# Part of block 1's front end and block 2's statistics issued inside the hand-ordered head of a Mamba + MoE kernel, with a new table of ranks

## The chip, the cores and the metric

The kernel runs on one core of one Trainium2 chip. The metric is the device time of one execution in microseconds (us). One execution is also recorded by the hardware profiler; its span, from the first to the last instruction, is what the profile's times are counted from.

The engines are called as the profile calls them: PE multiplies matrices (PEld is its weight load, which overlaps), DVE is the vector engine, ACT the scalar engine, POOL the GpSimd engine, SP the queue that issues most DMAs.

## What is computed

The input x has 4 sequences of 512 tokens with 256 features, all float32. In short:

```
x = x + layernorm(mamba(layernorm(x)))
x = x + layernorm(moe(layernorm(x)))

mamba(h):   xi, gate = split(h @ in_proj)                 # 512 channels each
            xi  = silu(causal_conv4(xi) + b)
            ts, B, C = split(xi @ x_proj)                 # 16, 16, 16
            dt  = softplus(ts @ dt_proj + dt_b)           # 512 channels
            s_t = s_{t-1} * exp(dt_t * A) + dt_t * B_t * xi_t   # 512 channels x 16 states
            y_t = sum_state(s_t * C_t)
            return ((y + D * xi) * silu(gate)) @ out_proj

moe(h):     top 4 of 16 experts by softmax(h @ w_router), weights renormalised
            out = shared/5 + (4/5) * sum_e cw_e * (silu(h@we1_e) * (h@we3_e)) @ we2_e
```

The kernel computes every expert for every token and multiplies by a weight that is zero for the experts not chosen; the shared network is cut into 4 more "experts" of the same size, so there are 20 of 128 hidden units each.

## The kernel before

**Blocks.** The 2048 tokens are cut into 8 blocks of 256 (n = 0 to 7); two blocks make one sequence, so the odd blocks continue the state and the convolution of the block before. Every block goes through four parts.

- The front (function front): statistics of x on DVE, reciprocal deviation on POOL (rstd_of, L380: four small instructions), normalisation on ACT (two instructions, L391), transposes on PE and their eviction on ACT, the projections `in` (two halves m = 0, 1) and `gin` (the gate, two halves), the convolution as matmuls with diagonal weights (`conv`), sigmoid on ACT and silu on DVE, `x_proj`, `ssm`, `dt`, softplus on ACT (a table load before and after it), and the DMAs that spread dt and dt*x over the layout of the scan.
- The scan: 32 slots per block, numbered k = 0 to 255 over all blocks. A slot has `exps` on ACT (three instructions), `scan` (L824) and `hc` (L832) on DVE and, in even blocks, `keep` on ACT. Every second slot has one `dbx` on POOL (L541). Every four slots have one `sum` on PE: 8 matmuls at L846 that read the four `hc` tiles. Two sums fill one PSUM tile, then `close` on DVE (L858) reads it.
- The chain: output projection (`out0`, `out`), layer norm, residual, second layer norm, transposes, router, top 4, and a DMA of the expert weights. It lies on all engines in turn.
- The experts, two at a time, 10 sets per block, numbered i = 0 to 79 over all blocks: `h1` and `h3` (4 matmuls each, L1088), `act` on ACT, `gated` on DVE (L1107), `weighted` and `product` on POOL, and `down` (4 matmuls, L1123).

**Who orders the work.** Each engine runs its instructions in the order in which the program issues them. The first part of the program is written out by hand: DMA issues, then function first() (L545 to L620), which takes block 0 as far as the inputs of slots 0 to 3. Everything after that is a list of tasks that class Plan puts in order with its own durations and dependencies. A task's rank is its nominal place plus a shift from the table SHIFTS (by kind and block) plus an entry of NUDGES (by task); PATIENCE lets a task of better rank go ahead of one that could start sooner. So the three tables decide the order of every engine from there on. Work that first() has already done is told to the planner with did(), with the buffers that it holds.

**Fillers.** warm(n, bank) issues n matmuls of a 128x128 identity that nobody reads. There are 20 at the start, 8 in the rest of first() (4 and 2 around x_proj, 2 before the spread at L607), and until the first `down` one group before each PE task whose planned start is late:

```python
spare_n = int((t["start"] - end - 0.4) / 0.22)
if early and spare_n > 1:
    warm(spare_n, "po")
```

**Buffers that matter here.** PSUM has three banks `h` for the scan (ps_e) and one each for f, y, h1, h3, po. In SBUF the ring `g` (3 buffers, 128x512) belongs to the experts, `o` (1 buffer) to the chain, `hc` has 11 buffers, `dbx` 3.

Of the kernel before, what the change touches and what calls it, by code (L numbers as in the profile page):

```python
# [14 lines left out]
P = 128  # L15
# [42 lines left out]
    fA=(-2, -14.75, -1.5, -59.5, 52, 5.75, 37.75, 15),  # L58
    fB=(20.5, -5, 12.5, 6.25, 26.25, 45.25, 0, -46),
    fC=(7.75, 2, -31, -1.5, 13.5, 14, -33.5, 18),  # L60
    fD=(12, 34.75, 16.5, 0.25, -2.5, 39.25, 8, 11.25),
    exps=(5.75, 36.5, 17.25, -3.75, -60, 51.75, 2, 37.75),
    dbx=(6.5, 1.25, -27.75, -13.5, -14.25, 5.25, 14.25, 46.5),
    scan=(33.75, 18.75, -5.75, 40.75, 52.75, 51.5, 57.25, -15.75),
    hc=(-4.75, -60, 50.25, -27, 28.5, 59.25, 16.75, 26.75),
    keep=(58, 0, -5.75, 0, 52, 0, 14.5, 0),
    sum=(60, -12.75, 1.25, 31.25, 16.5, 7, 0.5, -43.25),
    close=(-4.75, 27.5, 5.5, -13.75, -3, 20, 15, 36.5),
    ld=(1.5, 29.25, 27, -3, 15.75, -7.5, 57.5, -5.25),
    bc=(5, 3, 5.25, 6, 10.5, 15.75, 0.75, -3.25),  # L70
    chain=(-26, -5.25, -55, -60, -6, -38.25, -22.75, 0.25),
    load=(-5.5, 34, -50.25, 21.25, -21.25, -44, 2.75, 5.5),
    h1=(45.5, 3, -35.75, 8.25, 25.75, -0.5, 14.75, 34.5),
    h3=(11.25, -3, -53.5, -26, -29.25, -19, -15.75, -4),
    act=(-6.25, 40.25, 5.5, -11.5, -31.5, 0, 0, -3.25),
    gated=(-2, -9.5, -4.5, -23.25, 11.75, -60, -3, 0),
    prod=(33, -50, 58.75, -60, -50.75, -26.25, -8.75, 0),
    down=(-18.75, 25.5, -45, 42.25, -60, -14, 0.75, 37),
    fin=(14.75, -3, 27.75, 59, 0.5, 59.5, 3.5, -4),
# [3 lines left out]
    fA=(1.5, 0.1, 0.1, 0.3, 0.1, 1, 0.3, 0.1),  # L83
    fB=(2.2, 0.1, 0.1, 0.3, 0.1, 2.2, 0.6, 0.6),
    fC=(0.3, 0.1, 0.3, 1, 0.1, 0.6, 0.3, 0.3),
    fD=(2.2, 0.1, 0.1, 0.1, 0.1, 0.1, 0.1, 0.6),
    exps=(0.1, 0.1, 0.6, 0.1, 1.5, 0.3, 1.5, 0.3),
    dbx=(0.1, 0.3, 0.1, 0.1, 0.1, 0.1, 1, 1.5),
    scan=(0.1, 0.1, 0.1, 0.6, 0.1, 0.1, 0.1, 0.1),
    hc=(0.1, 0.1, 0.6, 1.5, 2.2, 0.1, 2.2, 0.1),  # L90
    keep=(0.1, 0.1, 0.1, 0.1, 0.6, 0.1, 0.1, 0.1),
    sum=(2.2, 0.1, 0.1, 0.1, 2.2, 0.1, 0.1, 0.1),
    close=(0.1, 0.1, 0.6, 1, 0.3, 0.3, 0.6, 1.5),
    ld=(1.5, 0.3, 1.5, 0.3, 0.1, 0.1, 0.1, 1.5),
    bc=(0.6, 0.1, 0.1, 1, 1, 0.1, 0.1, 0.3),
    chain=(0.6, 0.6, 0.1, 0.6, 0.6, 1, 0.1, 2.2),
    load=(2.2, 1, 0.6, 1, 2.2, 2.2, 0.6, 0.1),
    h1=(0.3, 0.3, 0.3, 0.1, 0.1, 0.1, 0.3, 0.1),
    h3=(0.1, 0.3, 2.2, 0.1, 0.1, 1, 0.6, 0.1),
    act=(0.6, 2.2, 0.1, 0.3, 0.1, 0.1, 0.6, 2.2),  # L100
    gated=(0.6, 0.3, 1, 0.1, 0.6, 0.1, 0.1, 1),
    prod=(2.2, 0.1, 0.1, 0.1, 0.1, 0.3, 0.1, 1.5),
    down=(0.1, 0.1, 0.1, 1.5, 0.1, 0.3, 0.1, 0.3),
    fin=(0.3, 0.3, 0.1, 1.5, 0.1, 1, 1, 0.3),
# [3 lines left out]
    ("gin", 0, 0): 5.5, ("pad0", 1, 0): 5.75, ("in", 1, 0): 3, ("xg", 1, 0, 1): 8,  # L108
    ("inputs", 1, 0): 8, ("gate", 1, 0): 14.5, ("evict", 2): 16.5, ("conv", 2, 1): -5.5,
    ("inputs", 2, 0): -27.75, ("pad0", 3, 1): -8, ("conv", 3, 1): 19.25, ("silu", 3, 1): -21.25,  # L110
    ("conv", 4, 0): 25, ("xg", 4, 0, 1): 7.5, ("gin", 4, 1): -27, ("gsig", 4, 1): 18.25,
    ("gate", 4, 1): 9.75, ("x_proj", 5): -1, ("in", 6, 1): -19.75, ("stats", 7): 5.5,
    ("conv", 7, 1): -22.5, ("x_proj", 7): 9.5, ("gin", 7, 0): 12.5, ("dbx", 2): -10,
    ("keep", 6): -14.25, ("keep", 9): -3, ("hc", 11): -1.75, ("keep", 11): -2.5,
    ("keep", 13): 13, ("dbx", 8): 32.75, ("keep", 16): -12, ("keep", 20): -21.25,
    ("scan", 21): 7, ("close", 6): -6, ("decay0", 7): -5, ("sum", 14): -3, ("yg", 7): -0.5,
    ("reps", 10): 12.5, ("hc", 84): 12.75, ("exps", 95): 10, ("exps", 96): -6.25,
    ("scan", 99): -7.75, ("sum", 24): -3, ("decay0", 13): 9.5, ("scan", 106): -3,
    ("sum", 27): -10, ("scan", 112): -14.75, ("scan", 118): 62, ("scan", 122): -3.5,
    ("scan", 125): -6.25, ("scan", 126): 2, ("scan", 138): -8.75, ("keep", 140): -4.75,  # L120
    ("scan", 144): 2.25, ("keep", 146): 27.25, ("scan", 157): 5.75, ("scan", 162): 23.25,
    ("dbx", 84): -4.75, ("decay0", 22): 4.5, ("scan", 179): 53.75, ("dbx", 91): 8.75,
    ("yg", 22): 57, ("scan", 196): -17.5, ("scan", 201): -0.25, ("reps", 26): 6,
    ("scan", 210): 11.25, ("scan", 214): -9, ("scan", 217): 6, ("sum", 54): 3.25,
    ("dbx", 110): -13, ("scan", 223): -8, ("delta", 28): 8.5, ("yg", 28): 24.5,
    ("scan", 235): -2.75, ("close", 29): 8, ("scan", 246): 48.75, ("scan", 252): -1.25,
    ("out0", 0): 35.5, ("rstd2", 0): -27.5, ("w13", 2): -3.75, ("cwb", 2): 15.75,
    ("h3", 3): 26.5, ("w13", 5): 14.75, ("product", 5): -7, ("w2", 6): -15, ("w13", 7): 4,
    ("gated", 7): -2, ("cwb", 9): 19, ("frstd", 0): -20.75, ("fadd", 0): 9.75,
    ("turnw", 1): 8.25, ("w13", 10): -12, ("h1", 10): 11.5, ("act", 15): -17.75,  # L130
    ("weighted", 17): -31.75, ("h3", 18): 3, ("down", 25): 17.75, ("cwb", 26): 10.75,
    ("down", 28): -9, ("h1", 29): -12.75, ("h1", 31): 8, ("down", 33): -14.5,
    ("act", 37): 15.25, ("add1", 4): 13.5, ("act", 46): -14.5, ("w13", 48): 9.5,
    ("share", 5): -10.75, ("cwb", 53): -4, ("h3", 54): 19, ("cwb", 54): -27.5,
    ("down", 54): -5.75, ("w2", 55): 2, ("h1", 55): -5, ("w2", 56): 2.5, ("w2", 58): 16,
    ("cwb", 59): -7.25, ("add1", 6): 8, ("down", 63): 15, ("h1", 67): -13.5, ("h1", 79): 3.25,
    ("fstats", 7, 1): -5, ("fadd", 7, 0): 8.75,
# [143 lines left out]
def mamba_then_moe(ctx: ExitStack, tc: tile.TileContext, a: dict, out: bass.AP):  # L281
# [17 lines left out]
    def load_x(n, what=xs, nm="x"):  # L299
        what[n] = work.tile([P, NU, D], F32, name=nm, bufs=RINGS[nm])  # L300
        nc.sync.dma_start(out=what[n], in_=x_in[:, n])
# [8 lines left out]
    nc.sync.dma_start(out=chan, in_=a["chan"].rearrange("(c p) k -> p c k", p=P))  # L310
    w_x = const.tile([P, CI, P // 2], F32, name="w_x")
# [17 lines left out]
    for n in range(1, 3):  # L329
        load_x(n)  # L330
# [92 lines left out]
    def in_proj(n, m, bank):  # L423
        t = q["in", n, m] = ps.tile([P, 2, U], F32, name=bank)
        for j in range(2):
            for k in range(CD):
                T.matmul(  # L427
                    t[:, j, :], w_in[:, k, ts(2 * m + j, P)], q["xn_t", n][:, k, :],
                    start=k == 0, stop=k == CD - 1,
                )  # L430

# [113 lines left out]
    def first():  # L545
# [5 lines left out]
        for i in range(NU):  # L551
            V.tensor_scalar(
                xn[:, i, :], xs[0][:, i, :], st[:, i, 1:2], rstd[:, i : i + 1],
                ALU.subtract, ALU.mult,
            )
        xn_t = q["xn_t", 0] = ring(work, [P, CD, U], "xn_t")
# [5 lines left out]
        make_taps()  # L562
        for m in range(2):
            in_proj(0, m, ("h3", "y")[m])
# [7 lines left out]
        for m in range(2):  # L572
            conv(0, m, (("po", "f"), ("h1", "h3"))[m])
        sigmoid(0, 0)
        silu(0, 0)

# [5 lines left out]
        silu(0, 1)  # L582
        S.activation(spare, zero, AF.Softplus)
        x_proj(0, "y", lambda c: warm(5 - c, "f"))
# [10 lines left out]
        warm(2, "y")  # L595
# [46 lines left out]
    for m in range(2):  # L642
        add(("xg", 0, 0, m), "SP", 0.9, 4.0 + m, lambda m=m: to_xg(0, 0, m, q["xt", 0, m]),
            (), (), [("xt", 0, m)], 256)
    did(("bc", 0), [("bt", ("bt", 0)), ("ct", ("ct", 0))])
# [9 lines left out]
    def front(n, at, over):  # L655
# [8 lines left out]
        def key(nm, *m):  # L664
            return (nm, n) + m
# [16 lines left out]
        if n:  # L682
# [3 lines left out]
            def stats():  # L686
                mine["mv"] = stats_of(xs[n])
# [28 lines left out]

            def pad0(m):
                xp = q["pad", n, m] = ring(work, [P, 2, KC - 1 + U], "xp")
                if n % UB:
                    G.tensor_copy(xp[:, :, 0 : KC - 1], tails.pop((n, m)))  # L720
                else:
                    G.memset(xp[:, :, 0 : KC - 1], 0.0)
# [7 lines left out]
            for m in range(2):  # L730
                ends = (n + 1) % UB
                starts = n % UB
                once(key("pad0", m), "POOL", 0.12, lambda m=m: pad0(m),
                     [("tail", n - 1, m)] if starts else [], [("xp", key("xp", m))],
                     [("tail", n, m)] if starts else [])
# [590 lines left out]
```

## Time and profile before

| | |
|---|---|
| median of 4 runs | 694.47 us (694.02 to 694.68) |
| profiled execution, its own time | 694.6 us |
| span of the profiled execution | 692.5 us |
| busy: PE / DVE / POOL / ACT | 675.7 / 578.2 / 602.3 / 493.4 us |
| first scan starts, first expert matmul starts | 27.71 us, 120.00 us |
| last matmul ends | 687.5 us |
| one group of 4 expert matmuls (two records each) | 1.73 us |
| one scan; one hc, busy | 1220 ns; 680 ns |

A busy PE is not a PE that does needed work: the fillers count as busy, too (216 records for 108 of them at L349 in banks f and po, and 4 for 2 in bank y). Matmul records overlap, so the pace is read from one group's start to the next. The DMAs of 256 KB land some 4.5 us after their issue, most of them hidden.

### The profile page before, as it was taken

What the parts mean: (1) busy time and instruction counts of PE and PEld (TensorE: products, weight loads), DVE (VectorE), ACT (ScalarE), POOL (GpSimd) and SP (SyncE); (2) the same over time, 40 slices, a digit from 0 to 9 for tenths busy, and PEclk for the clock granted to TensorE, in tenths of its full rate; (3) what the DMA queues carried; (4) which work ended last, traced back from release to release, by engine and by line L of the source; (5) the groups of instructions that cost most, each with busy time, mean ns of one, the idle gap of its engine ahead of it and who ended that gap; (6) DMA issues with size and microseconds to landing.
All of it is one profiled execution on the core that took longest, in us unless ns stands there. A gap on an engine that the chain in (4) does not pass through costs nothing.

```text
span 692.5 us, 13366 instructions
## 1 busy us (share of the span) xinstructions
PE 675.7 (98%) x4480; PEld 539.5 (78%) x4480; DVE 578.2 (83%) x821; ACT 493.4 (71%) x1308; POOL 602.3 (87%) x607
## 2 busy tenths in 40 slices
PE   8999998999999999999999999999999999999997
PEld 7876776767878678887787787787877787888886
DVE  3698999999999899999999999889999979952112
ACT  2799979988778778877798857877778657733311
POOL 1598669999999999999999999999999999985553
PEclk9999999999999999999999999999999999999999
DMA  5397765586866686777668766788776656463560
GB/s 175 115 337 241 258 238 191 191 268 199 288 233 222 211 303 215 232 262 279 217 226 279 245 222 226 213 291 288 244 245 227 235 192 213 139 228 131 189 228 29
DMA packets 84840, 155.28 MB, mean 224 GB/s; under 512 B 9858, under 2 KB 33410, under 8 KB 84772
## 3 DMA queue, kind: packets, MB, share of 16 engines
q1 hardware_dynamic: 83940, 153.13, 65.8%
q10 hardware_dynamic: 832, 1.31, 0.5%
q8 instruction: 35, 0.57, 0.3%
q14 instruction: 33, 0.27, 0.1%
HBM read 135.40 MB, written 19.01 MB: 223 GB/s over the span
## 4 chain that ended last, share of the span: by engine, by line
PE 62%; DVE 13%; ACT 10%; POOL 8%; DMA 3%; issue 3%; SPq 0%; DVEq 0%; POOLq 0%
PE h L1088 30%; PE po L1123 14%; DVE h L824 6%; PE y L846 6%; POOL dbx L541 4%; ACT h L529 4%; DVE hc L832 3%; PE f L941 3%; PE f L427 2%; PE f L442 2%; PE f L1123 1%; PE f L349 1%; DMA xg<-gate 1%; DVE gate L786 1%; POOL g L1110 1%
## 5 line engine op out<-in xcount | busy, mean ns | idle before, releaser
L824 DVE TENSOR_TENSOR_SCAN h<-h,dbx 128x512 f32<-128x512 f32 x256 | 307.4, 1220 | 11.7 <-ACT h L532 5.9
L541 POOL TENSOR_TENSOR dbx<-rep,bt 128x1024 f32<-128x1024 f32 x127 | 300.1, 2366 | 12.6 <-DVE h L824 12.4
L1088 PE MATMUL h<-xn_t,w 128*128 128x256 f32 x1280 | 295.2, 382 | 0.1
L529 ACT ACTIVATE h<-rep,a_rep 128x256 f32<-128x256 f32 x512 | 244.6, 478 | 53.2 <-DVE hc L832 41.4
L1088 PEld LDWEIGHTS h<-xn_t,w 128*128 128x128 f32 x1280 | 239.5, 190 | 42.7 <-issue 4.0
L832 DVE TENSOR_TENSOR hc<-h,ct 128x512 f32<-128x512 f32 x256 | 169.9, 680 | 2.9 <-ACT carry L836 0.7
L1123 PE MATMUL po<-w,g 128*128 128x256 f32 x600 | 143.7, 382 | 1.0 <-POOL g L1110 1.0
L1123 PEld LDWEIGHTS po<-w,g 128*128 128x128 f32 x600 | 111.7, 190 | 22.3 <-POOL g L1110 3.7
L1110 POOL TENSOR_TENSOR g<-g,q 128x512 f32<-128x512 f32 x80 | 102.0, 1274 | 9.0 <-DVE q L1107 7.1
L1107 DVE SCALAR_TENSOR_TENSOR q<-th,h 128x512 f32<-128x512 f32 x80 | 54.4, 680 | 49.5 <-PE h L1088 41.2
L1103 POOL TENSOR_TENSOR g<-g,cwb 128x512 f32<-128x512 f32 x64 | 81.7, 1276 | 14.5 <-ACT g L1100 13.9
L1095 ACT ACTIVATE th<-h 128x512 f32<-128x512 f32 x80 | 47.6, 595 | 46.7 <-PE h L1088 46.5
L846 PE MATMUL y<-hc,sel 128*32 128x256 f32 x1024 | 67.7, 385 | 0.0
L846 PEld LDWEIGHTS y<-hc,sel 128*32 128x32 f32 x1024 | 27.4, 109 | 28.6 <-issue 14.5
L532 ACT COPY h<-zero 128x1 f32<-128x1 f32 x256 | 41.7, 163 | 8.2
L427 PE MATMUL f<-xn_t,w_in 128*128 128x256 f32 x176 | 42.5, 384 | 1.6 <-DVE gate L786 1.1
L1100 ACT COPY g<-h 128x512 f32<-128x512 f32 x64 | 37.1, 580 | 8.7 <-PE f L1123 8.7
L427 PEld LDWEIGHTS f<-xn_t,w_in 128*128 128x128 f32 x176 | 32.7, 190 | 9.1 <-DVE gate L786 1.7
L836 ACT COPY carry<-h 128x2 f32<-128x2 f32 x128 | 19.6, 159 | 15.3 <-DVE hc L832 7.6
L442 PE MATMUL h<-xp,taps 64*64 64x256 f32 x288 | 29.5, 381 | 0.8 <-DVE xt L459 0.8
L941 PE MATMUL f<-w_out,yg 128*128 128x256 f32 x112 | 26.7, 384 | 0.2 <-DVE xt L459 0.2
L442 PE MATMUL f<-xp,taps 64*64 64x256 f32 x208 | 25.3, 382 | 0.7 <-DVE gate L786 0.4
(178 smaller groups left out, 631.4 us busy)
## 6 DMA issues: line engine op xcount, KB each, us to landing
w<-in_w SPq DMA_DIRECT2D x80, 512.0 KB, 4.8
rep<-rep SPq DMA_DIRECT2D x124, 256.0 KB, 4.5
w<-in_w SPq DMA_DIRECT2D x80, 256.0 KB, 4.5
cwb<-cwd SPq DMA_DIRECT2D x64, 256.0 KB, 4.9
xg<-xg SPq DMA_DIRECT2D x32, 256.0 KB, 4.7
bt<-bc SPq DMA_DIRECT2D x8, 512.0 KB, 6.0
ct<-bc SPq DMA_DIRECT2D x8, 512.0 KB, 6.2
xg<-gate SPq DMA_DIRECT2D x16, 256.0 KB, 4.3
```

The costliest lines, as they stand in the source:

```text
L427: T.matmul(t[:, j, :], w_in[:, k, ts(2 * m + j, P)], q["xn_t", n][:, k, :], start=k == 0, stop=k == CD - 1,)
L442: T.matmul(t[j][half[r ^ j], :], taps[half[r], 2 * m + j, k, :], q["pad", n, m][half[r], j, k : k + U], start=k == 0, stop=k == KC - 1,)
L529: S.activation(h[:, j, :], dt[:, m, 0, :], AF.Exp, scale=a_rep[:, c, g, m : m + 1])
L541: G.tensor_tensor(t[:, m], reps[n * CI + c][:, m, 1, :], bt[:, m], ALU.mult)
L824: V.tensor_tensor_scan(flat, flat, dbx[:, ts(p, NJ), :].rearrange("p j t -> p (j t)"), 0.0, ALU.mult, ALU.add)
L832: V.tensor_tensor(hc, expo[k], ct, ALU.mult)
L846: T.matmul(ys[n, c][m * CS : (m + 1) * CS, :], sel, hcs[k][:, j, :], start=g == 0, stop=g == SG - 1,)
L1088: T.matmul(t[:, j, :], weights[i][:, j, ts(CD * w + k, P)], x[:, k, :], start=k == 0, stop=k == CD - 1,)
L1103: G.tensor_tensor(gs[i], gs[i], cws[i], ALU.mult)
L1107: V.scalar_tensor_tensor(t, hid[i, "th"], 1.0, hid[i, 1], ALU.add, ALU.mult)
L1110: G.tensor_tensor(gs[i], gs[i], hid[i, "q"], ALU.mult)
L1123: T.matmul(acc[n][t] if n == N - 1 else acc[n][:, t, :], gs[i][:, j, ts(t, P)], weights2[i][:, j, :], start=m == 0 and j == 0 and (t == 0 ...
```

## The change

Four things are edited by hand, and the three tables (SHIFTS, PATIENCE, NUDGES) are replaced as a whole.

1. The load of block 1's x is issued third on SP, ahead of four loads of weights, where it was ninth.
2. first() now also does, for block 1: statistics (DVE), reciprocal deviation (POOL), normalisation (ACT), transposes (PE) into an `h` bank, their eviction on DVE (it was ACT) into a buffer of ring `g`, the projection `in` half 0 (PE; two matmuls in the place of four fillers between the halves of x_proj, two in the place of two fillers behind dt's projection), its copy into the padded tile on DVE (it was ACT), and the two copies of the convolution's tail on POOL. It also takes block 2's statistics (DVE).
3. These tasks leave the planned part: for block 1 stats, rstd, norm, transpose, evict, both pad0, in half 0 and its copy; for block 2 the task stats stays but issues nothing.
4. The number of fillers is 109 where it was 110: 22 in the hand-written part (28 before) and 87 in the planned part (82 before).

The counts of matmuls other than fillers are the same in both programs. The orders of all engines behind first() differ throughout, since the tables differ.

```diff
 SHIFTS = dict(
...
-    scan=(33.75, 18.75, -5.75, 40.75, 52.75, 51.5, 57.25, -15.75),
+    scan=(30.75, 59, -4.25, 58.25, 59, 55.75, 19.5, -8.5),
...
-    sum=(60, -12.75, 1.25, 31.25, 16.5, 7, 0.5, -43.25),
+    sum=(-4.75, 3.5, -4.5, 1.5, 11.75, 24.5, -21.25, 0.5),
...
@@ the DMA issues ahead of the program
     nc.sync.dma_start(out=chan, in_=a["chan"].rearrange("(c p) k -> p c k", p=P))
+    load_x(1)
     w_x = const.tile([P, CI, P // 2], F32, name="w_x")
...
-    for n in range(1, 3):
-        load_x(n)
+    load_x(2)
...
-    def in_proj(n, m, bank):
-        t = q["in", n, m] = ps.tile([P, 2, U], F32, name=bank)
+    def in_parts(n, m, t):
+
+        q["in", n, m] = t
         for j in range(2):
             for k in range(CD):
                 T.matmul(
                     t[:, j, :], w_in[:, k, ts(2 * m + j, P)], q["xn_t", n][:, k, :],
                     start=k == 0, stop=k == CD - 1,
                 )
+                yield
+
+    def in_proj(n, m, bank):
+        for _ in in_parts(n, m, ps.tile([P, 2, U], F32, name=bank)):
+            pass
...
@@ first()
+
+        mr = rstd_of(stats_of(xs[1]))
         xn_t = q["xn_t", 0] = ring(work, [P, CD, U], "xn_t")
...
         make_taps()
+        xn1 = ring(work, [P, NU, D], "o")
+        normalize(xn1, tiles_of(xs[1]), mr)
...
         for m in range(2):
             conv(0, m, (("po", "f"), ("h1", "h3"))[m])
+        t = ps_e.tile([P, CD, U], F32, name="h")
+        for k in range(CD):
+            for i in range(NU):
+                T.transpose(t[:, k, ts(i, P)], xn1[:, i, ts(k, P)], ident)
         sigmoid(0, 0)
         silu(0, 0)
+
+        q["xn_t", 1] = ring(work, [P, CD, U], "g")
+        V.tensor_copy(q["xn_t", 1], t)
...
         silu(0, 1)
+
+        live[2]["mv"] = stats_of(xs[2])
+        parts = in_parts(1, 0, ps_e.tile([P, 2, U], F32, name="h"))
+        for m in range(2):
+            xp = q["pad", 1, m] = ring(work, [P, 2, KC - 1 + U], "xp")
+            G.tensor_copy(xp[:, :, 0 : KC - 1], tails.pop((1, m)))
+
+        def some(c):
+            if c == 1:
+                next(parts)
+                next(parts)
+            else:
+                warm(2, "f")
+
         S.activation(spare, zero, AF.Softplus)
-        x_proj(0, "y", lambda c: warm(5 - c, "f"))
+        x_proj(0, "y", some)
...
         V.tensor_copy(first_b, b0)
-        warm(2, "y")
+        for _ in parts:
+            pass
+        V.tensor_copy(q["pad", 1, 0][:, :, KC - 1 :], q["in", 1, 0])
         softplus(0)
...
+    did(("evict", 1), [("g", ("xn_t", 1))], eng="DVE")
+    for m in range(2):
+        did(("pad0", 1, m), [("xp", ("xp", 1, m))], [("tail", 1, m)], eng="POOL")
+    did(("tail", 1, 0), (), [("xp", 1, 0)], eng="DVE")
...
@@ front(n, at, over)
-        if n:
+        if n > 1:
...
             def stats():
-                mine["mv"] = stats_of(xs[n])
+                mine["mv"] = live[n].get("mv") or stats_of(xs[n])
...
-            for m in range(2):
+            for m in range(n == 1, 2):
```

## The prediction

> **What bounds the kernel now.** I read the page first, then the busy time by stage, then PE and DVE in order of time through the head and at one place in the middle. The page:
>
> ```profile
> span 692.5 us, 13366 instructions
> PE 675.7 (98%) x4480; PEld 539.5 (78%) x4480; DVE 578.2 (83%) x821; ACT 493.4 (71%) x1308; POOL 602.3 (87%) x607
> ```
>
> PE is idle for 16.8 us of the span. Its busy time holds fillers, so it says only this: with equal needed matmuls and 109 fillers for 110, the changed kernel's PE is busy for as long as before within 0.2 us, and the time can move only by what happens to these 16.8 us. Busy time by stage, cut at the end of the head's spread (26.29), slot 4 (36.69), slot 31 (94.77), slot 40 (115.84), the first expert matmul (120.00), the end of hc 115 (290.62) and sum 28 (297.78):
>
> ```profile
> 26.29:36.69 10.40, 8.95 (x71) 7.73 (x69) 10.02 (x15) 8.05 (x23) 9.70 (x11) 1.00 0.49 159
> 36.69:94.77 58.08, 55.08 (x552) 42.15 (x544) 55.66 (x74) 52.52 (x151) 44.62 (x42) 1.00 0.80 272
> 94.77:115.84 21.07, 19.17 (x135) 15.12 (x129) 19.78 (x26) 18.25 (x45) 18.02 (x26) 1.00 0.57 200
> 115.84:120.00 4.16, 3.48 (x34) 2.37 (x33) 4.16 (x7) 3.73 (x13) 3.84 (x9) 1.00 0.92 303
> 297.78:385.00 87.22, 85.77 (x583) 67.78 (x583) 83.05 (x112) 70.60 (x196) 85.86 (x77) 1.00 0.75 253
> 385.00:687.50 302.50, 302.43 (x1769) 246.13 (x1767) 225.75 (x319) 185.58 (x486) 263.61 (x263) 1.00 0.63 212
> 115.84:290.62 174.78, 173.02 (x1164) 134.38 (x1164) 165.06 (x235) 140.93 (x374) 168.89 (x169) 1.00 0.70 235
> ```
>
> The columns are length, then busy time of PE, PEld, DVE, ACT and POOL, granted clock, DMA. Before 120 us the scan sets the pace: DVE is idle for 2.4 of 58 us from slot 4 to slot 31, and PE is kept busy by 82 fillers of about 0.24 us (18 records in 2.17 us) and still waits 7.0 us. After 120 PE sets the pace, waiting 2.6 us in all (1.1 to 298, 1.4 to 385, 0.1 after), but DVE is close behind: of 174.8 us it is idle for 9.7. From the last matmul to the end it is 5.0 us, which the change does not touch.
>
> **The head, row by row.** PE, then DVE:
>
> ```profile
> 18.07 1.16 PE L349 MATMUL f<-ident 128*128 128x128 f32 x8
> 19.16 0.66 PE L470 MATMUL y<-xt,w_x 128*64 128x128 f32 x8
> 22.03 0.61 PE L349 MATMUL y<-ident 128*128 128x128 f32 x4
> 22.76 1.10 PE L607 MATMUL f<-dt,w 128*128 128x256 f32 x4
> ```
>
> ```profile
> 17.57 0.28 DVE L580 TENSOR_SCALAR sig<-sig 128x256 f32<-128x256 f32 x1
> 17.95 0.88 DVE L459 SCALAR_TENSOR_TENSOR xt<-h,chan,sig 128x256 f32<-128x256 f32 x2
> 27.09 0.70 DVE L377 BATCH_NORM_STATS2 st<-x 128x6 f32<-128x512 f32 x1
> 27.71 2.33 DVE L824 TENSOR_TENSOR_SCAN h<-h,dbx 128x512 f32<-128x512 f32 x2
> ```
>
> The statistics of block 1 (0.62 by their step) fit into DVE's idle 8.1 to 9.4, the POOL chain (1.47 where it now stands) into its idle time, the normalisation (1.09) on ACT between 10.4 and the copy at 11.63, the transposes (0.65) on PE behind the convolution at 16.9. The eviction is the first that does not fit: it stands on DVE ahead of L580 and waits for the transposes, so L580 starts at about 18.4 and the second silu ends at 19.6, 0.8 later. PE's second x_proj half, at 19.16, then starts its last part at 19.85 and ends some 0.5 later than before, and the bias copy, dt and softplus follow. Behind dt the two remaining matmuls of the projection (0.87, by 1.73 for four) replace two fillers (0.61). So the spread starts at about 23.45 for 22.76: **+0.7**. DVE's copy of the projection (0.69) fits in its idle time before the first spread copy, and block 2's statistics (0.62) in the idle time behind the second silu (3.4 us before). POOL's u, dbx 0, u and dbx 1 hang on the spread and come 0.7 later. Against this DVE loses stats 1 at 27.09 and stats 2 (0.6 each), and POOL loses rstd 1 (1.47) and two tail copies (0.33) ahead of dbx 2. By these steps slot 2 starts at 32.45 (31.73 before, held by dbx 1), and slot 4 at 36.55 (36.69 before). ACT's norm, evict and copy (1.09, 0.58, 0.59) leave a stretch where ACT is idle anyhow. On SP the load put third delays four weight loads by one issue (0.5) and 256 KB, about 0.8 us at the 330 GB/s moved there; they are needed 9 us later or more. DMA costs nothing unless that load is late (a rival below).
>
> **Slot 4 to the first expert matmul.** In the order of the two programs DVE has the same number of scans, hc, gates, silu, close and stats between slots 4 and 40. ACT does not: by exps 37 it has done softplus three times where it was once (before, softplus 2 follows one slot later and softplus 3 behind the first experts). What one costs:
>
> ```profile
> 60.35 1.28 ACT L499 ACT_TABLE_LOAD   x1
> 62.75 1.28 ACT L529 ACT_TABLE_LOAD   x1
> ```
>
> ```profile
> 65.26 1.23 DVE L824 TENSOR_TENSOR_SCAN h<-h,dbx 128x512 f32<-128x512 f32 x1 [1.26 <-ACT h L532]
> ```
>
> Each of the two such times before slot 40 in this trace costs DVE one wait of 1.2 to 1.3 us (at 65.26 and 113.97); a third makes slot 40 about +1.1 (0.14 gained, 1.26 lost). Bounds: 1.5 earlier, if better order removes the two waits instead, and 2.4 later, if each costs double.
>
> [...]
>
> The chain of block 0: stats1 stands about 0.9 later on DVE, rstd2 is relieved on POOL of a dbx (2.36) for small work of about 0.5, and conv (4, 0), 1.9 us, replaces 0.9 of fillers ahead of h1 0. That sums to +0.0, so h1 0 stays at 120. PE's fillers and matmuls alone allow 114; late ACT work can make it 121.5. By then PE has done, of the 2.2 us moved (1.73 and 0.47 to 0.65), 1.3 more than before, since the planned part has 0.9 less done (in, gin and transposes fewer, conv and dt more). If nothing else changed, the end would be **1.3 earlier**.
>
> **The middle.** In the order of before, sum 28 has on PE 24 h1, 24 h3 and 22 down ahead of it; in the changed order 20, 20 and 19, and all else in the planned part is equal. That is 11 groups of 1.73 us: **19.0 us** less. Its last input, hc 115, has on DVE two `gated` fewer and one stats fewer ahead of it. Measured before:
>
> ```profile
> 297.78 1.07 PE L846 MATMUL y<-hc,sel 128*32 128x256 f32 x16
> ```
>
> ```profile
> 289.93 0.69 DVE L832 TENSOR_TENSOR hc<-h,ct 128x512 f32<-128x512 f32 x1
> ```
>
> Sum 28 had 7.2 us to spare. Now: hc 115 ends at 290.6, plus 1.1 (slot 40), minus 0.6 (between slot 40 and there: two `gated` out, one stats in), minus r, what DVE gains from its 9.7 us of idle time. With the shortest way from hc to sum in the trace (0.15), sum 28 starts at 291.3 - r. After it PE has 19.0 more to do, less the 2.2 done in the head: 16.8. So the end moves by 291.3 + 16.8 - 297.8 = **10.3 - r**. For r I take the waits of DVE on PE, 3.7 us (`close` 1.9, `gated` 1.4, stats 0.4): PE's side now comes earlier than DVE's. Of the other 6.0 (waits on exps 2.3, the rest short) I take half, since no row says which go: r = 6.7 and **+3.6**. Its bounds are 3.7 (+6.6) and 9.7 (+0.6). The neighbours point the same way: by the same working sum 20 gives +3.8 and sum 33 +3.4, each less its own r. PE executes in order, so experts behind a waiting sum wait too.
>
> The sum against the profiled execution's own 694.6 us (2.1 over the span, 0.1 over the median): 694.6 + 3.6 = **698.2**.
>
> **Rivals.**
>
> Faster: DVE gains all 9.7 us and slot 40 is 1.5 earlier, not 1.1 later. Then 10.3 - 9.7 - 2.6 = -2.0, the pinch no longer decides, and the 1.3 is kept with most of the 1.1 us of PE waits between 120 and 298: about 692.2. For it: DVE's order has fewer tasks on others' heels, and a planner's order spread over all engines may remove waits that a row cannot show. Against: exps wait on slots and softplus, which no order takes away. It decides from r + (slot 40's gain) above 10.3.
>
> No change: the pinch costs what the head gives, 694.6, when r is near 10 with slot 40 unmoved or the change does to PE's waits nothing at all.
>
> Late load: block 1's x lands after 8.7 us; then its statistics hold up DVE's eviction at 9.39 and with it all that follows. The load of 128 KB now third landed at 7.63; 128 KB more at 330 GB/s make 8.0. The next landing behind it was a_rep at 10.51: +1.8 at most, on top of any case.
>
> **Chances and range.** Pinch and slower 0.53, late load 0.05 (on its own 696.4), no change 0.12, faster 0.30. Within 0.2% is 693.1 to 695.9, about what a measurement tells from no change: slower 0.58, same 0.12, faster 0.30. The low end is the faster case with all 2.6 us of PE's waits after 120 gone and 0.2 of fillers: 694.6 - 1.3 - 2.6 - 0.2 = 690.5. The high end is +6.6 with slot 40 a further 1.3 late: 702.5. The likeliest case alone has 696 to 702.5.
>
> **What would show it.** In the profile after: the spread at 23.4 and not 22.8; slot 4 near 36.5; a third softplus ahead of slot 40 with a DVE wait of over 1 us on exps; h1 0 within 1.5 us of 120; PE waiting at L846's group for hc between 200 and 350 us, more than 5 us in all, where it now waits under 0.1; the granted clock at 1.00 throughout. The prediction is wrong if DVE's idle time there falls under 3 us, or if PE's waits stay under 3 us after 120.

## The result, and the profile after

The changed kernel takes 695.41 us (median of 37 runs, 694.07 to 697.09); the kernel before, timed beside it, 694.20 (55 runs, 693.58 to 694.94). The ratio is 1.0016, 95% interval [1.0011, 1.0021]: slower by 0.16%, some 1.2 us. The forecast was slower by 3.6. Its sign was right and its range holds the time, but its size is three times too large.

The profiled execution took 694.94 us by its own time, over a span of 693.2. Around the span lie 1.8 us now and 2.1 before (2.0 to 2.2), in every execution of the two: 0.3 us of the loss of span is given back there. The page's head:

```profile
span 693.2 us, 13378 instructions
PE 677.2 (98%) x4478; PEld 539.6 (78%) x4478; DVE 578.0 (83%) x823; ACT 492.7 (71%) x1306; POOL 602.2 (87%) x607
```

PE's idle time fell, from 16.8 to 16.0 us, while the kernel became slower. Its busy time rose by 1.5 us with one filler fewer. The records show how that can be: a group of four 128x256 matmuls (eight records) shows 1.89 us where the next group starts 1.73 later, and up to 1.99 where the next starts 1.83 later. So short waits can hide inside PE's busy time, and its gaps are not all of its waits; how much of the 1.5 us is of this kind was not counted.

Busy time by stage, cut where the forecast cut it (end of the spread, slot 4, slot 31, slot 40, first expert matmul; then sum 28 to 385, to the last matmul, and slot 40 to the end of hc 115). Columns: stretch, length, then busy time of PE, PEld, DVE, ACT and POOL, granted clock, DMA share, GB/s.

```profile
26.24:35.80 9.56, 9.26 (x77) 7.19 (x77) 9.12 (x12) 7.44 (x21) 9.10 (x7) 1.00 0.47 154
35.80:95.09 59.29, 54.97 (x527) 41.16 (x522) 57.53 (x75) 55.11 (x152) 44.70 (x42) 1.00 0.84 287
95.09:115.04 19.95, 18.64 (x149) 14.83 (x147) 19.52 (x27) 18.27 (x47) 18.38 (x30) 1.00 0.66 222
115.04:118.96 3.92, 3.92 (x57) 2.51 (x56) 3.92 (x7) 3.76 (x13) 3.84 (x5) 1.00 0.69 239
281.31:385.00 103.69, 102.62 (x690) 80.86 (x689) 95.38 (x127) 85.18 (x230) 101.63 (x90) 1.00 0.78 254
385.00:688.00 303.00, 302.89 (x1739) 248.35 (x1737) 220.26 (x314) 181.29 (x470) 260.85 (x260) 1.00 0.63 211
115.04:281.64 166.60, 164.91 (x1123) 127.47 (x1124) 161.64 (x234) 134.20 (x368) 161.29 (x161) 1.00 0.67 229
```

From slot 40 to hc 115 DVE's busy time fell from 165.06 to 161.64 and its idle time from 9.72 to 4.96. POOL is as full there as DVE: three engines, not one, are within a few per cent of full. Between 281 and 385 us POOL is busy for 101.6 of 103.7, DVE for 95.4.

The head, PE and then DVE:

```profile
17.14 0.69 PE L474 MATMUL y<-xt,w_x 128*64 128x128 f32 x8
19.05 0.66 PE L474 MATMUL y<-xt,w_x 128*64 128x128 f32 x8
21.92 1.03 PE L426 MATMUL h<-g,w_in 128*128 128x256 f32 x4
22.78 1.03 PE L638 MATMUL f<-dt,w 128*128 128x256 f32 x4
```

```profile
17.25 0.68 DVE L590 COPY g<-h 128x512 f32<-128x512 f32 x1
17.85 0.28 DVE L595 TENSOR_SCALAR sig<-sig 128x256 f32<-128x256 f32 x1
18.17 0.88 DVE L463 SCALAR_TENSOR_TENSOR xt<-h,chan,sig 128x256 f32<-128x256 f32 x2
27.05 1.22 DVE L862 TENSOR_TENSOR_SCAN h<-h,dbx 128x512 f32<-128x512 f32 x1
```

The spread starts at 22.78 as before, not at 23.45. But the two profiles don't start alike: PE's first transposes of the normalised x start at 8.70 us in the profile before, right behind the 20 fillers of the start, which end at 8.64, and anywhere from 7.86 to 9.07 in fourteen profiles with this head (at 8.26 in the first one after, where they wait 0.23 us for DVE's xn); what follows shifts with them. So I measure from there. "After" has two profiles, the second from the run after_again below.

| us behind the first transposes | before | after | after, second profile |
|---|---|---|---|
| first transposes, from the span's start | 8.70 | 8.26 | 8.96 |
| spread | 14.06 | 14.52 | 14.40 |
| scan of slot 4 | 27.99 | 27.54 | 27.42 |
| scan of slot 10 | 39.46 | 41.13 | 41.46 |
| scan of slot 40 | 107.14 | 106.78 | 107.34 |
| first expert matmul | 111.31 | 110.70 | 111.27 |
| start of hc 115 | 281.23 | 272.69 | 273.27 |
| sum 28 | 289.08 | 273.05 | 273.61 |
| sum 63, the last | 608.57 | 607.86 | 608.42 |
| last group of matmuls | 676.92 | 677.83 | 678.40 |

The first projection on PE (L426) starts 0.90 us behind the first transposes in the profile before and in the second one after, 1.02 in the first: so 0.12 of the first profile's column lies ahead of anything that the change touches. The last line is +0.9 and +1.5, +1.2 in the mean. Behind the last matmul the changed order puts `fmean` of one half ahead of `fstats` of the other on DVE: 5.2 us to the end for 5.0. With 0.2 there and 0.3 less around the span, 1.1 is what the medians show.

The pinch that the forecast was built on, sum 28 and its last input, PE and then DVE:

```profile
281.31 1.07 PE L884 MATMUL y<-hc,sel 128*32 128x256 f32 x16
```

```profile
280.96 0.68 DVE L870 TENSOR_TENSOR hc<-h,ct 128x512 f32<-128x512 f32 x1
```

It is there: sum 28 starts while hc 115 still runs, with no slack, where it had 7.2 us before.

### The profile page after: what moved, and what is told of

Its sections match the earlier page's. It is cut to its first block, busy times and chain, and to the rows that moved or that the text cites. A ratio compares the mean times of both kernels' runs of the same rounds, so it can differ in the third digit from the quotient of the medians.

```text
span 693.2 us, 13378 instructions
## 1 busy us (share of the span) xinstructions
PE 677.2 (98%) x4478; PEld 539.6 (78%) x4478; DVE 578.0 (83%) x823; ACT 492.7 (71%) x1306; POOL 602.2 (87%) x607
## 4 chain that ended last, share of the span: by engine, by line
PE 59%; ACT 10%; DVE 10%; POOL 8%; DMA 7%; issue 3%; SPq 2%; POOLq 0%; DVEq 0%; ACTq 0%
PE h L1126 30%; PE po L1161 13%; PE y L884 5%; ACT h L533 4%; DVE h L862 4%; POOL dbx L545 4%; PE f L979 3%; DVE hc L870 3%; PE f L426 2%; DMA rep<-rep 2%; DMA w<-in_w 2%; POOL g L1148 2%; PE f L1161 1%; POOL g L1141 1%; DMA rep<-u 1%
## 5 line engine op out<-in xcount | busy, mean ns | idle before, releaser
L870 DVE TENSOR_TENSOR hc<-h,ct 128x512 f32<-128x512 f32 x256 | 171.9, 681 | 3.5 <-ACT carry L874 1.1
L426 PE MATMUL f<-xn_t,w_in 128*128 128x256 f32 x160 | 38.6, 384 | 0.8 <-ACT xn_t L739 0.4
L426 PEld LDWEIGHTS f<-xn_t,w_in 128*128 128x128 f32 x160 | 29.6, 190 | 7.1 <-ACT xn_t L739 0.6
```

What stands on the lines that cost most here:

```text
L426: T.matmul(t[:, j, :], w_in[:, k, ts(2 * m + j, P)], q["xn_t", n][:, k, :], start=k == 0, stop=k == CD - 1,)
L870: V.tensor_tensor(hc, expo[k], ct, ALU.mult)
```

## The experiments

Differences below are to the kernel before as timed beside each run; the changed kernel itself stands at +1.1 to +1.2. The intervals are mostly 1.2 to 2 us wide, so the trace carries most readings: between the two profiles of the changed kernel every stage behind slot 15 repeats to 0.05 us.

My first theory (A): the scan chain (DVE with ACT's exps and POOL) sets the pace and PE is carried along, so the 2.2 us of matmuls moved into the head buy nothing. The rival (B): PE sets the pace after 120 us, and the gain is lost in waits that the new order puts on PE.

**Table and edits apart.** The old table under the new edits, and the new table under the old code:

```
edits_old_table:     after.py with SHIFTS, PATIENCE, NUDGES of before.py
old_code_new_table:  before.py with SHIFTS, PATIENCE, NUDGES of after.py
```

> The edits in the head with the three tables of before. Theory A (the head's gain of about 2.2 us of PE work is real and is lost again behind it, by the order that the new table makes): 692.0 us, 2.2 under before, with PE's losses behind the head as in before. Theory B (the gain has no use, since the scan sets the pace until 120 us and DVE after it): 694 to 695, whatever the table.

> The code of before with the new tables. Theory A: the new order without the head's gain, 2.2 us over the changed kernel's 695.4: 697.6. Theory B: the table alone makes the difference, 695.4.

755.99 us, ratio 1.0886 [1.0871, 1.0900], and 742.38, ratio 1.0689 [1.0674, 1.0703]. Both expectations missed by far. Neither table serves the other's list of tasks, so these two runs can't judge edit and table apart, and no other run here does.

**A wait that the new order makes.** In the changed kernel the convolution (4, 0) stands ahead of the first experts and holds the bank that h3 of the first expert needs, until the silu on DVE has read it:

```profile
118.96 1.99 PE L1126 MATMUL h<-xn_t,w 128*128 128x256 f32 x8
120.80 1.50 PE L347 MATMUL po<-ident 128*128 128x128 f32 x12
122.71 1.99 PE L1126 MATMUL h<-xn_t,w 128*128 128x256 f32 x8 [0.41 <-DVE xt L463]
```

Fillers (L347) were planned into the wait; 2.0 us lie between the end of h1 0's work (1.73 us behind its start) and h3 0. The edit gives that convolution another bank:

```diff
-  conv(n, m, banks)
+  conv(n, m, ("f", "po") if (n, m) == (4, 0) else banks)
-  if early and spare_n > 1:
+  if early and spare_n > 1 and t["name"] != ("h3", 0):
```

> The changed kernel, its order untouched, with the second half of conv (4, 0) in bank po instead of h3, and without the one group of 6 fillers ahead of h3 0, so that h3 0 need not wait for silu (4, 0). Theory A (PE time lost behind 120 us never comes back): the 2.0 us lost before h3 0 go, 693.4. Theory B (the sums of the middle wait for DVE, so PE cannot use an earlier start): at most 0.5 us, 694.9 or more, with sum 14 or sum 28 waiting for its hc.

695.22 us, ratio 1.0012 [1.0003, 1.0021], +0.75. h3 0 follows h1 0 at once, and the next task waits instead, for POOL's routing weights:

```profile
119.34 3.72 PE L1126 MATMUL h<-xn_t,w 128*128 128x256 f32 x16
124.28 0.39 PE L1065 MATMUL h<-ident,cw 128*16 128x128 f32 x2 [1.21 <-POOL cw L1060]
```

By 140 us PE is where it was. The wait was real, and taking it away bought nothing at the end. That speaks for A.

**Without the planned fillers.**

```diff
-            if early and spare_n > 1:
-                warm(spare_n, "po")
```

> The changed kernel, its order untouched, without the 87 fillers of the planned part. If fillers only fill time in which PE would wait: 694.5 to 695.4, the granted clock still 1.00, PE idle about 21 us longer in the profile. If they keep the clock up: slower than 697, with a granted clock under 1 between 28 and 125 us.

697.35 us, ratio 1.0045 [1.0032, 1.0057], +2.9. The granted clock falls to 0.51 three times ahead of slot 40 (columns as above):

```profile
40.00:43.40 3.40, 1.42 (x25) 0.98 (x28) 3.40 (x5) 2.96 (x9) 3.16 (x7) 1.00 1.04 347
43.40:46.90 3.50, 3.50 (x32) 1.56 (x24) 3.43 (x6) 3.21 (x9) 3.22 (x3) 0.51 0.99 360
80.90:84.40 3.50, 3.50 (x9) 2.77 (x9) 3.26 (x5) 3.36 (x10) 3.26 (x7) 0.51 0.44 150
98.00:104.90 6.90, 6.90 (x41) 4.83 (x40) 5.43 (x7) 5.74 (x14) 5.63 (x9) 0.51 0.96 325
```

The same stretches with fillers stay at 1.00. From 80.9 to 84.4 us PE is busy throughout in both kernels, with 9 records at 0.51 and with 16 at 1.00, no filler among them. Slot 31 comes only 0.1 us later behind the first transposes than in the changed kernel's first profile, so the first two stretches cost the scans next to nothing; slot 40 comes 1.75 later. In the third stretch and just behind it DVE waits for PE's slower matmuls:

```profile
100.04 0.48 DVE L896 SCALAR_TENSOR_TENSOR xg<-xg,chan,y 128x256 f32<-128x256 f32 x1 [0.53 <-PE y L884]
105.39 0.70 DVE L375 BATCH_NORM_STATS2 st<-h 128x6 f32<-128x512 f32 x1 [1.44 <-PE h L979]
```

The last matmul comes 1.9 later: a delay ahead of slot 40 passes to the end whole. In the 3.40 us ahead of the first stretch PE was busy for 1.42, with the fillers for 2.76. Why the clock falls at these three places no run shows.

**The scans' own cost.** An hc directly behind its own scan starts 1.256 us after the scan's start; directly behind the scan of another slot, with its own further ahead, it starts 1.127 after that scan's start (medians over 66 and 62 such pairs; before: 1.256 and 1.127 too). The changed order has 24 pairs of the first kind ahead of slot 40, the one before 4. Ten of them parted:

```diff
+    FIRST = [(1, ("scan", 2)), (3, ("scan", 4)), (5, ("scan", 6)), (7, ("scan", 8)),
+             (9, ("scan", 10)), (13, ("stats", 3)), (14, ("scan", 15)), (15, ("scan", 16)),
+             (16, ("close", 1)), (30, ("scan", 31))]
+    for k, name in FIRST:
+        t = next(t for t in tasks if t["name"] == name)
+        tasks.remove(t)
+        tasks.insert(next(i for i, o in enumerate(tasks) if o["name"] == ("hc", k)), t)
```

> The changed kernel with ten DVE instructions of slots 2 to 31 (eight scans, stats 3, close 1) put ahead of the hc that stood right behind its own scan; nothing else moves. In the profile after, hc starts 1.256 us after its own scan's start when it follows it directly and 1.127 with another instruction between. Theory A (from 28 us on the scan chain sets the pace, and its shifts pass to the end one for one): ten pairs at 0.13 make slot 40 about 1.0 to 1.3 earlier than 115.04, the end with it, 694.1 to 694.4 for 695.4. Theory A2 (ACT's exps set the pace of the slots ahead of 40): slot 31 up to 1.0 earlier but slot 40 within 0.3 of 115.04, and 695.1 to 695.5. Theory B (PE's order sets the end after 120 us): 695.3 to 695.5 whatever slot 40 does.

699.17 us, ratio 1.0069 [1.0056, 1.0081], +4.7: all theories missed, and the sign too. Slot 4 is 0.5 later behind the first transposes, slot 40 3.9, the last matmul 4.1. ACT and DVE wait for each other more (columns: total, times, longest). In this kernel, from 28 to 75 us:

```profile
ACT carry L874 <- DVE hc L870: 6.4, 6, 2.5
DVE gate L824 <- ACT sig L820: 3.0, 4, 1.4
```

In the changed kernel, from 28 to 72 us:

```profile
ACT carry L874 <- DVE hc L870: 2.3, 4, 0.8
DVE gate L824 <- ACT sig L820: 0.4, 2, 0.2
```

Putting a scan ahead of an hc saves 0.13 us on DVE, but the hc comes a scan later (1.2 us). ACT waits for it at `carry`, the copy that `keep` makes, and what stands behind the copy in ACT's order comes later too. DVE pays for that at the gates, which need a sigmoid from ACT, and hardly at the exps: it waits 0.4 us for them here and 0.2 in the changed kernel. Why the copy waits for the hc, and not for its scan alone, was not tested. For these ten together adjacency is the cheaper order, and what I had taken for a loss of the new table was not one.

**Loads of ACT's tables.** The third softplus ahead of slot 40 was the forecast's +1.26.

```diff
-  AF.Softplus
+  AF.Exp if 0 < n < 4 else AF.Softplus
```

> The changed kernel with the softplus of blocks 1 to 3 replaced by Exp (other values, so other outputs; the same shapes and durations of work), which takes away ACT's loads of tables, two of 1.28 us for each of three blocks ahead of slot 40. Theory A2 (ACT's exps set the pace there): slot 40 earlier by 1.2 for each pair that DVE waits for, at least 1.2 and up to 3.8, all of it at the end: 691.6 to 694.2. Theory A with DVE alone setting the pace: slot 40 at most 0.5 earlier, since only one DVE wait on exps of over 1 us is left there, and 694.9 to 695.4. Theory B: no change at the end, 695.3 to 695.5.

695.17 us, ratio 1.0010 [1.0001, 1.0019], +0.7. ACT is busy for 485.7 us instead of 492.7, with six loads of 1.28 us fewer. From slot 4 to slot 40 it takes 79.1 us, for 79.2 and 79.9 in the two profiles of the changed kernel. All three softplus together cost the scans 0.1 to 0.8 us, not 1.26 each: DVE's largest wait for exps from 36 us to slot 40 shrank from the first of these lines (before) to the second (after).

```profile
DVE h L824 <- ACT h L532: 2.5, 2, 1.3
```

```profile
DVE h L862 <- ACT h L536: 0.8, 3, 0.3
```

Six loads are 7.7 us by their own time; ACT's busy time fell by 7.0, and slot 40 hardly moved. A load has 10 to 20 ns on either side, in the kernel before (at 60.35 and 62.75 us) and in the changed one (at 53.60 and 56.00).

**Taking work from PE and adding it, at one place.** Three runs ask what a microsecond is worth on PE and DVE at about 200 us (the "eight matmuls" of the expectations are eight records, that is four matmuls):

```diff
pe_less_200:   -  for k in range(CD)                    # h1, h3 of group 11: 4 of 8 matmuls
               +  for k in range(1 if i == 11 else CD)
pe_more_200:   -  for j in range(EB)                    # h1 of group 11: 4 matmuls twice
               +  for j in list(range(EB)) * 2
dve_more_200:  -  V.tensor_tensor(hc, expo[k], ct, ALU.mult)
               +  three times for k == 74
```

> The changed kernel with expert group 11 (at 201 us) summed over half of its inputs in h1 and h3: eight matmuls, 1.73 us of PE's work, are left out, nothing else moves. Theory A (the scan chain sets the pace, PE is carried along): hc 115 and sum 28 within 0.3 of 281.6 and 281.3, the end 695.0 to 695.4. Theory B (after 120 us PE's work sets the end): 693.5 to 693.9, and sum 28 waits 1.7 for hc 115 or hc 115 moves with it.

> The changed kernel with hc 74 (at 194 us) computed three times, 1.38 us more on DVE, nothing else moved. Theory A: hc 115 0.8 to 1.4 later than 281.64, sum 28 with it, and the end 696.1 to 696.8. Theory B: DVE's idle time between 194 and 282 us (part of the 5.0) takes most of it: hc 115 at most 0.5 later, the end 695.3 to 695.9.

Less on PE: 695.43 us, ratio 1.0017 [1.0008, 1.0026], +1.0; in the trace every engine is back on the changed kernel's times by 211 us. More on DVE: 696.48, ratio 1.0036 [1.0022, 1.0050], +2.0; the 1.4 us are still there at hc 115 (+1.3) and at the last matmul (+1.3). Where PE's 1.73 us went:

```profile
201.87 1.03 PE L1127 MATMUL h<-xn_t,w 128*128 128x256 f32 x4
203.45 1.99 PE L426 MATMUL f<-xn_t,w_in 128*128 128x256 f32 x8 [0.55 <-ACT carry L874]
205.28 1.03 PE L1127 MATMUL h<-xn_t,w 128*128 128x256 f32 x4
207.04 1.99 PE L1162 MATMUL po<-w,g 128*128 128x256 f32 x8 [0.72 <-POOL g L1149]
```

Into two waits that the changed kernel doesn't show, for ACT and for POOL's product. This is what A expects, but A also says that PE has time to spare. A new theory (L): in this filled order all engines run in step; a delay on any of them passes on, and an engine that gets ahead waits for the next. It has to show two things: that more work on PE costs too, and that it goes on behind sum 28, where the forecast (P below) let PE's work alone decide.

> The changed kernel with the eight matmuls of h1 of expert group 11 (at 201 us) done twice, 1.73 us more on PE, nothing else moved. Theory L (up to the pinch at sum 28, 281 us, PE and DVE run in step: in a filled order a delay on either passes on, an earlier engine waits for the other): hc 115 and the end 1.2 to 1.7 later, 696.6 to 697.1. Theory A (PE is carried along with time to spare): at most 0.5 later, 695.3 to 695.9.

697.00 us, ratio 1.0045 [1.0032, 1.0057], +2.7: 1.4 later at hc 115, 1.3 at the last matmul. PE delays the expert's tanh on ACT, ACT the exps behind it, and so the scan:

```profile
209.03 1.23 DVE L862 TENSOR_TENSOR_SCAN h<-h,dbx 128x512 f32<-128x512 f32 x1 [1.62 <-ACT h L536]
```

A falls with this, and L stands. Behind sum 28, with the same edits on groups 27 and 47 and on hc 136:

> The changed kernel with expert group 27 (at 333 us, behind the pinch at sum 28) summed over half of its inputs in h1 and h3, 1.73 us of PE's work left out. Theory P (behind sum 28 PE's work alone sets the end): 693.5 to 693.9, hc 255 up to 1.7 earlier too. Theory S (the scan chain sets the pace until its last slot at 614): 695.1 to 695.5, hc 255 within 0.3. Theory L (in step there as well): as S.

> The changed kernel with expert group 47 (at 490 us) summed over half of its inputs in h1 and h3, 1.73 us of PE's work left out. Theory P: 693.5 to 693.9. Theories S and L: 695.1 to 695.5.

> The changed kernel with hc 136 (at 331 us) computed three times, 1.38 us more on DVE. Theory P: DVE, busy for 226 of the 303 us behind 385, takes it up: hc 255 and the end at most 0.4 later, 695.3 to 695.8. Theories S and L: hc 255 and the end 1.2 to 1.5 later, 696.5 to 696.9.

695.08 us, ratio 1.0011 [1.0002, 1.0020], +0.8; 695.36, ratio 1.0015 [1.0007, 1.0024], +1.1; and 696.31, ratio 1.0036 [1.0023, 1.0050], +2.05. In the traces the two with less PE work gain 0.25 and 0.07 us of 1.73 between their place and the last matmul, and the one with more on DVE loses 1.1 of 1.38. P falls. The gain at 333 us goes to POOL's products, and the one at 490 to a gate on DVE whose bank the next transposes need:

```profile
334.99 1.99 PE L1162 MATMUL po<-w,g 128*128 128x256 f32 x8 [0.73 <-POOL g L1149]
340.57 1.99 PE L1162 MATMUL po<-w,g 128*128 128x256 f32 x8 [0.34 <-POOL g L1149]
```

```profile
494.31 0.66 PE L1009 MATMUL f<-ident,xn 128*128 128x128 f32 x4 [1.75 <-DVE gate L824]
```

**Behind the last scan, the head's eviction, and the changed kernel once more.**

```diff
pe_less_650:        as pe_less_200, for group 74
evict_behind_silu:  -  V.tensor_copy(q["xn_t", 1], t)      # ahead of sigmoid and silu (0, 1)
                    +  the same behind silu(0, 1); in_parts(1, 0) reads q["xn_t", 0]
after_again:        no edit
```

> The changed kernel with expert group 74 (at 653 us, behind the last scan) summed over half of its inputs in h1 and h3, 1.73 us of PE's work left out. Theory L (in step up to the last scan at 614 us, PE alone behind it): the last matmul 1.5 to 1.7 earlier, 693.5 to 693.9. If down 74 or a later group waits for the product on POOL there too: 695.0 to 695.4.

> The changed kernel with DVE's eviction of block 1's transposes put behind the head's second silu; so that PE does not wait for it, the first half of block 1's projection reads block 0's normalised input instead (other values). If the eviction on DVE is what the head costs: from the first transposes to the spread 14.1 us as in the kernel before, for 14.4 to 14.5 in the runs of the changed one, slot 4 0.3 earlier behind the first transposes too (27.2 for 27.55). If ACT's half of the sigmoid sets it: 14.4 still. At the end, theory L with the head ahead of everything: 0.3 earlier, 695.0 to 695.2; if later waits swallow it, 695.3 to 695.5.

> The changed kernel once more, timed beside the others and profiled a second time. Theory L: 695.2 to 695.6, and from the first transposes to slot 4, slot 40, sum 28 and the last matmul the times of its first profile (27.55, 106.8, 273.05, 679.7) within 0.3, so that the difference to the kernel before, measured from the first transposes, is +0.9 at the last matmul; if the first profile was favoured by chance, 0.3 to 0.5 more from slot 10 on, as in two of the other runs.

Less PE work behind the last scan: 694.53 us, ratio 1.0004 [0.9994, 1.0013], +0.4. From sum 63 to the last group of matmuls it is 68.8 us instead of 70.0: 1.15 of the 1.73 count, and the rest went to a wait for ACT and shorter ones. The longest wait:

```profile
655.55 3.72 PE L1127 MATMUL h<-xn_t,w 128*128 128x256 f32 x16 [0.30 <-ACT g L1139]
```

Of the four places tried, only the one in these last 74 us has PE's time worth most of itself.

The eviction behind the silu: 694.97, ratio 1.0009 [1.0000, 1.0018], +0.85. From the first transposes to the spread it is 14.29 us, where the changed kernel has 14.40 to 14.52 and the one before 14.06. Measured from the first projection, which leaves out the 0.12 of chance ahead of it (this run has it too), it is 13.27 us, where both profiles of the changed kernel have 13.50 and the one before 13.16. So the eviction on DVE costs 0.23 of the head's 0.34, and its absence reaches slot 4 as 0.23 (26.29 for 26.52). At the end 0.2 can't be told.

The changed kernel again: 695.25, ratio 1.0017 [1.0007, 1.0026], +1.1. Its second profile is the last column of the table above: 0.6 later from slot 40 on than the first, all of it lost between slots 4 and 15. The place is dbx 4, which waits for a load of `rep`; POOL's wait in the second profile, between 26 and 45 us:

```profile
POOL dbx L545 <- DMA rep<-rep: 1.7, 1, 1.7
```

In the first profile the wait ahead of dbx 4 is 1.0 us (put down there to a silu on DVE, which dbx 4 doesn't read); the silu and scans around it keep their times. In the eleven profiles that share the order up to there and have no other delay, dbx 4 starts 29.5 to 30.6 us behind the first transposes and slot 15 52.5 to 53.3 us, later with it. So the start of dbx 4, most likely by this load, decides up to 0.8 us of a single execution. It may be why the changed kernel's times spread wider (3.0 us, for 1.4 before); that was not tested.

No version beat the kernel before.

## Why the prediction was right or wrong

**The bound (PE's idle time is all that can move): wrong.** PE's idle time shrank while the time grew, its busy time rose by 1.5 us where the forecast had it equal within 0.2, and 1.73 us taken from PE at 201, 333 or 490 us were worth 0.25 at most in the traces. After 120 us and up to the last scan no single engine set the pace. "After 120 PE sets the pace ... but DVE is close behind" read the busy shares as a ranking; where PE, DVE and POOL are all busy for 90% or more (from 119 to 614 us) and run fixed orders, each step waits for another engine somewhere.

**The head (+0.7): too large.** The spread is 0.35 to 0.45 later behind the first transposes, 0.34 behind the first projection. The eviction, charged with 0.5, costs 0.23: the second silu ends 0.53 later, but before the change PE stood in fillers for 0.3 us behind the end of that silu, and this slack took the rest. The projection's two matmuls, charged with 0.26 over the fillers, take 0.86 to the start of the spread where the fillers took 0.73. Slot 4, forecast at -0.14, came out at -0.5.

**Slot 40 (+1.1): the term that failed first.** It is -0.1 in the mean of two profiles. Its content, one DVE wait of 1.26 for every softplus, fell with softplus_as_exp. The two waits of before were waits for exps in that order, not the price of a load.

**First expert at 120: held** (118.96), **and PE's 1.3 us ahead: true and worthless.** Two us went at h3 0, which the forecast didn't see: it counted the order's work but not who holds the bank.

**The middle (10.3 - r, r = 6.7, where r is what DVE gains from its idle time): the sum held and two sizes were off.** From slot 40 to the end of hc 115 it took 166.6 for 174.8, so r was 7.6, within its bounds. Sum 28 starts 0.3 ahead of hc 115's end, not 0.15 behind it: 0.5. From sum 28 to the last matmul the changed kernel needs 16.9 us more; 16.8 was forecast. So 3.6 - 1.2 (slot 40) - 0.9 (r) - 0.5 + 0.1 = 1.1, and 1.2 was measured at the last matmul. The failing step in the prediction's words is "makes slot 40 about +1.1" (measured -0.1), and then "r = 6.7" (measured 7.6).

That the arithmetic closes doesn't make its cause right. The forecast let PE's remaining work decide because PE alone was the bound behind sum 28; the runs at 333 and 490 us refute that. That 16.9 us came out where 16.8 were forecast is then no proof of the step, and the right sign is in part luck; a guess, not tested, is that the planner filled both orders to about the same degree. Read at the other end the same +1.2 is: the last sum comes 0.4 us earlier (mean of the two profiles), and behind it 38 expert groups stand in the order (11 h1, 13 h3, 14 down) where there were 37, and PE needs 1.6 us more there. One group is 1.73. The run that takes a group's worth of work away at 653 us bears this out: it stands at +0.4, and the interval of its ratio holds 1. Why the new order leaves one more group behind the last sum stays open.

**PE waiting at sums for hc, over 5 us: not seen.** PE's waits from the first expert matmul to the last matmul are 2.9 us, for 2.6 before, none of them at a sum; the condition named for "wrong" (under 3) was met. The longer ones, from 120 to 688 us:

```profile
PE h L1126 <- DVE xt L463: 1.5, 3, 0.6
PE f L446 <- ACT carry L874: 0.6, 1, 0.6
PE po L1161 <- POOL g L1148: 0.4, 2, 0.2
```

The clock stayed at 1.00, as said, in every stretch up to the last matmul. The load of x1 came in time: its statistics start at 8.36 us, directly behind DVE's xn of block 0.

**No change by cancelling** was given 0.12, with 693.1 to 695.9 us counted as no change. 695.41 lies in that band and nearer to it than to the forecast; that it is slower at all can be told only from 37 and 55 runs.

## What to carry to other kernels

Before costing a move in a kernel where several engines are over 90% busy, ask what a microsecond is worth on each of them at that place: repeat an instruction there, then leave one out. Ahead of the last scan a repeated one cost some 75 to 95% of itself here and a missing one gained almost nothing, so work moved into an idle stretch of PE in the head bought nothing at the end. Compare two profiles from an event behind the start-up loads, and take a second profile before explaining half a microsecond.

## What was not expected of the hardware

- An hc directly behind the scan whose result it reads starts 1.256 us after that scan's start, directly behind another slot's scan 1.127 after that one's: a difference of 0.13 us.
- With the 87 planned fillers left out the granted clock fell to 0.51 for 3.5, 3.5 and 6.9 us, from 43.4, 80.9 and 98.0 us on; in the 3.40 us ahead of the first PE was busy for 1.42. With the fillers it was 1.00 there.
- The first transposes start at 7.86 to 9.07 us in fourteen profiles with the same head, and dbx 4, which in one of them waits 1.65 us for a load, 29.5 to 30.6 us behind them in eleven; what lies around the span is 1.8 us for the changed kernel and 2.1 for the one before, and no run says why.
